# A perceiver block on one core: the first attention's maximum and sum spread by float32r matmuls, and weight buffers arranged anew

## The chip, the cores and the metric

The kernel runs on one core of one Trainium2 chip, in one launch. The core has TensorE (matmuls, written PE in the profile; PEld is its loading of the stationary operand), VectorE (DVE), ScalarE (ACT), GpSimd (POOL) and SyncE (SP), which issues the transfers here; each works through its own queue in order. The metric is the time of one execution on the device in microseconds (us). The kernel before takes 2688.52 us, the median of three runs (2685.12 to 2690.39).

## The reference

Two layers of three blocks each work on `x` (8 batches of 64 rows, 512 wide) and a context `ctx` (8 batches of 1601 rows, 512 wide), all in float32:

```python
x = x + xattn0(layernorm(x), ctx)   # 32 query heads, 8 key/value heads, head size 128, learned Wq, Wkv, Wo
x = x + mamba(layernorm(x))         # selective scan, 1024 channels, 16 states
x = x + ternary_ffn(layernorm(x))
x = x + xattn1(layernorm(x), ctx)   # softmax(x ctx^T) ctx, no weights
x = x + attn1(layernorm(x))         # causal self-attention, 32 heads of 16
x = x + oct_ffn(layernorm(x))       # gated, ternary octonion weights
```

The first block is where nearly all of the work lies. For a batch and one of the 8 key/value heads (a *unit* from here on) it is

```python
k, v   = ctx @ Wk + bk, ctx @ Wv + bv                 # 1601 x 128 each
scores = q @ k.T / sqrt(128)                          # 4 query heads x 64 rows = 256 queries
attn   = softmax(scores)                              # over 1601 keys
o      = attn @ v ;  out = o @ Wo + bo
```

## The kernel before

**Precision.** TensorE takes two kinds of four-byte operand here, float32 (`FP`) and float32r (`FR`), of the same size in memory. Where float32r is used, a value is kept as two float32r halves: `split` (L100) writes hi with a ScalarE copy that rounds, and lo = value - hi with VectorE or GpSimd. A product then has three terms (hi hi, hi lo, lo hi). Keys, values, scores and Wo are done so; the weighted sum over the values (L464), the maximum's spread (L412) and the sum's spread (L472) use plain float32.

**The main loop.** `x_all` (L517) goes through 64 units, batch by batch. Each unit has six steps. In them TensorE makes the keys of blocks of the context (`x_k`, L363) and the values of one tile of 128 context rows (`x_v`, L334), and the scores, transposed: keys on the partitions, the 256 queries along the free axis (`x_s`, L385). The softmax of a unit runs during the next unit's steps:

- `x_max` (step 0): the running maximum over the key tiles is transposed (L403), reduced by VectorE to one negative maximum per query (`col`, tile `mc`, L405).
- `x_spread` (step 0): two matmuls of 128 columns with `col` broadcast as the stationary side and the identity as the moving one bring each query's maximum to all partitions (L412).
- `x_exp` (steps 0 to 4, seven calls): VectorE adds the spread maximum to a pair of score tiles (L426), ScalarE takes the exponential (L427), GpSimd adds the pair to the running sum `ss` (L429, L452). The last call adds the short thirteenth tile (L446) and folds the two halves into `sl` (L448). For the very last unit (`flush`) VectorE does a part of it (L434 to L442).
- `x_av` (steps 2 to 5): the exponentials times the values, in plain float32 (L464).
- `x_o` (step 5): a matmul of 256 columns with a matrix of ones sums `sl` over the partitions and spreads the sum (L472); ScalarE and VectorE form the reciprocal (L474 to L477), scale (L479) and split the result.
- `x_wo`: for odd batches, the product with Wo (L511), weights fetched in four tiles per unit on the tag `wo` (three buffers).

The PSUM tag `kv` has four banks (`KVB`), shared by keys, values, scores and Wo; `o` and `m` have one each.

**The side work.** Beside the main loop run generators, advanced in step with it (`advance`, L1314): `halves` (L606) splits Wo, W_out and the attention weights once and stores the halves in HBM (56 tiles, during the first batch); `prep` (L620) makes ternary weights; and `chain` (L761), one for each group of two batches, does the other five blocks. While the main loop runs, what these issue on VectorE, ScalarE and GpSimd is kept in program order; the rest is ordered by the framework's scheduler, with its own model of durations. SyncE's queue issues the transfers in order, so a transfer that waits for a buffer holds those behind it.

**The tail.** The last group's chain starts when the main loop is done; the pools of the main loop and of the Mamba blocks (`ca`) are closed and their room is used by larger buffers (`BUFS_TAIL`), which wait for what was there. The third group's chain is still running then.

**Buffers that the diff touches** (`BUFS`, L46): `lv` (4 KB a partition) holds the Mamba block's u, dt and dus; `w2` (2 KB) single halves of weights for `mm3` (L742), which does the three terms; `b2` temporaries, among them the three pieces of a row of scores in `xattn1` (L1011), of 512, 512 and 578 columns; `b2` takes the size of the largest.

Of the kernel before, what the change touches and what calls it, by code (L numbers as in the profile page):

```python
# [16 lines left out]
P = 128  # L17
# [25 lines left out]
CPLAN = (0, 1, 2, None, None, 3)  # L43
AVPLAN = ((), (), (0, 1, 2, 3), (4, 5, 6, 7), (8, 9, 10, 11), (12,))
EXPLAN = ((0,), (1, 2), (3,), (4, 5), (6,), ())
BUFS = {"a2": 5, "lv": 3, "bc": 1, "xpad": 1, "b2": 5, "b4": 2, "w2": 3, "xr": 2}  # L46
BUFS_TAIL = {"a2": 6, "du": 2, "bc": 2, "xpad": 4, "s4": 11, "kb": 3, "b2": 8, "b4": 3, "w2": 12, "xr": 2}


# [29 lines left out]
class Kernel:  # L79
# [317 lines left out]
    def x_max(self, b, i):  # L397

        nc = self.nc
        m = self.mf.pop((b, i))  # L400
        ps = self.px.tile([P, 2, 256], FP, name=self.nm("m_ps"), tag="m", bufs=MB)
        for h in range(2):
            nc.tensor.transpose(ps[:, 0, h * P : (h + 1) * P], m[:, 0, h * P : (h + 1) * P], self.ident)  # L403
        col = self.sb("mc", [P, 2], pool=self.xp, bufs=2)
        nc.vector.tensor_reduce(col, ps[:, 0].rearrange("p (h k) -> p h k", k=P), AX.X, ALU.max, negate=True)  # L405
        self.mm[(b, i)] = (ps, col)

    def x_spread(self, b, i):

        ps, col = self.mm[(b, i)]  # L410
        for h in range(2):
            self.nc.tensor.matmul(  # L412
                ps[:, 1, h * P : (h + 1) * P], lhsT=col[:, h : h + 1].to_broadcast([P, P]), rhs=self.ident, start=True, stop=True
            )

    def x_exp(self, b, i, n):

        nc = self.nc
        ps = self.mm[(b, i)][0]
        S = self.S[(b, i)]  # L420
        if n == 0:
            self.ss[(b, i)] = self.sb("ss", [P, 2, 256], pool=self.xp, bufs=1)
        ss = self.ss[(b, i)]
        r, w = (P, 2) if n < 6 else (TAIL, 1)
        sv = S[n][:r, :w]
        nc.vector.tensor_tensor(sv, sv, ps[:r, 1:2].to_broadcast([r, w, 256]), ALU.add)  # L426
        nc.scalar.activation(sv, sv, AF.Exp, scale=ISC)  # L427
        if n == 1:
            nc.gpsimd.tensor_tensor(ss, S[0], S[1], ALU.add)  # L429
        elif n > 3 and self.flush:  # L430

            if n == 5:
                t = self.fs = self.sb("rw", [P, 256], pool=self.xp, bufs=1)
                nc.vector.tensor_tensor(t, S[4][:, 0], S[4][:, 1], ALU.add)  # L434
                for k in range(2):
                    nc.vector.tensor_tensor(t, t, S[5][:, k], ALU.add)
            elif n == 6:
                t = self.fs
                nc.vector.tensor_tensor(t[:r], t[:r], sv[:, 0], ALU.add)
                l = self.sb("sl", [P, 256], pool=self.xp, bufs=1)  # L440
                nc.vector.tensor_tensor(l, ss[:, 0], ss[:, 1], ALU.add)
                nc.vector.tensor_tensor(l, l, t, ALU.add)  # L442
                self.l[(b, i)] = l
                self.mm.pop((b, i))
        elif n == 6:
            nc.gpsimd.tensor_tensor(ss[:r, 0], ss[:r, 0], sv[:, 0], ALU.add)  # L446
            l = self.sb("sl", [P, 256], pool=self.xp, bufs=1)
            nc.gpsimd.tensor_tensor(l, ss[:, 0], ss[:, 1], ALU.add)  # L448
            self.l[(b, i)] = l
            self.mm.pop((b, i))  # L450
        elif n > 1:
            nc.gpsimd.tensor_tensor(ss, ss, S[n], ALU.add)  # L452
# [13 lines left out]
    def x_o(self, b, i):  # L466
# [2 lines left out]
        ps = self.o.pop((b, i))  # L469
        self.S.pop((b, i))  # L470
        r = self.l.pop((b, i))
        nc.tensor.matmul(ps[:, 1], lhsT=self.ones, rhs=r, start=True, stop=True)  # L472
# [19 lines left out]
    def x_wo(self, b, i):  # L492
# [113 lines left out]
    def halves(self):  # L606
# [2 lines left out]
        todo = [(i["Wo"][k * G + g], self.wo_s[k][:, g]) for k in range(NKV) for g in range(G)]  # L609
        todo += [(i["W_outT"][h], self.wout_s[h]) for h in range(NCH)]  # L610
        todo += [(i["attnT"][m, c], self.wat_s[m][c]) for m in range(4) for c in range(NC)]
        for src, dst in todo:
            t = self.sb("wo", [P, 2, D], FR, pool=self.xp, bufs=WOB)
            nc.sync.dma_start(out=t[:, 1].bitcast(FP), in_=src)
            yield 0.5
            self.split(t[:, 0], t[:, 1], t[:, 1].bitcast(FP), eng=nc.gpsimd)
            nc.sync.dma_start(out=dst, in_=t.bitcast(FP))
            yield 0.5

    def prep(self):  # L620
# [121 lines left out]
    def mm3(self, ps, lhsT, wt, N, start, stop, exact=False, tg="w2"):  # L742

        nc = self.nc
        if exact:
            wh = self.sb(tg, [P, D], FR)[:, :N]
            nc.sync.dma_start(out=wh.bitcast(FP), in_=wt)
        elif self.tail:
            w = self.sb(tg, [P, 2, D], FR)
            nc.sync.dma_start(out=w.bitcast(FP), in_=wt)  # L750
            wh, wl = w[:, 0], w[:, 1]
        else:
            wh, wl = (self.sb(tg, [P, D], FR) for _ in range(2))
            nc.sync.dma_start(out=wh.bitcast(FP), in_=wt[:, 0])
            nc.sync.dma_start(out=wl.bitcast(FP), in_=wt[:, 1])
        nc.tensor.matmul(ps, lhsT=lhsT(0), rhs=wh, start=start, stop=False)  # L756
# [240 lines left out]
    def xattn1(self, bs, x, xo):  # L997

        nc, i = self.nc, self.i
        lt = self.lnT(x, P, hl=False)  # L1000
        GW = [(0, (256, 256)), (1, (256, 256)), (2, (192, 192)), (2, (194,))]
        SW = [512, 512, 577]
        TS = ((0, 4), (4, 8), (8, NT))

        def scores(k, b):
# [2 lines left out]
                s = self.sb("bc", [T, LP])  # L1008
                S = [s[:, :512], s[:, 512:1024], s[:, 1024:]]
            else:  # L1010
                S = [self.sb("b2", [T, 512]), self.sb("b2", [T, 512]), self.sb("b2", [T, 578])]  # L1011
            o = 0
            for m, ws in GW:
                ps = self.acc()
# [20 lines left out]
                o += e  # L1035
                if not self.tail:
                    yield 2 * len(ws)
            nm = self.sb("s1m", [T, 4])
            for m in range(3):
                nc.vector.tensor_reduce(nm[:, m : m + 1], S[m][:, : SW[m]], AX.X, ALU.max)  # L1040
            nc.vector.tensor_reduce(nm[:, 3:4], nm[:, 0:3], AX.X, ALU.max, negate=True)
            sm2 = self.sb("s1s", [T, 4])
            for m in range(3):
                nc.scalar.activation(S[m][:, : SW[m]], S[m][:, : SW[m]], AF.Exp, bias=nm[:, 3:4], accum_out=sm2[:, m : m + 1])
            sm = sm2[:, 3:4]
            nc.vector.tensor_reduce(sm, sm2[:, 0:3], AX.X, ALU.add)
            nc.vector.reciprocal(sm, sm)
            yield 3
            return S, sm
# [1 line left out]
        def values(k, b, S, sm):  # L1051
            q0 = k * T
            pts = []
            for m, (t0, t1) in enumerate(TS):
                pt = self.sb("b2", [P, 5, T])
                tp = self.acc().rearrange("p (t q) -> p t q", q=T)
                for t in range(t0, t1):
                    r = rows_of(t)
                    nc.tensor.transpose(tp[:r, t - t0, :], S[m][:, (t - t0) * P : (t - t0) * P + r], self.ident[:T, :T])
# [225 lines left out]
    def run(self):  # L1285
# [3 lines left out]
        self.pc = ctx.enter_context(tc.tile_pool(name="pc", bufs=2, space=PSUM))  # L1289
        xctx = ctx.enter_context(ExitStack())  # L1290
        self.px = xctx.enter_context(tc.tile_pool(name="px", bufs=2, space=PSUM))
        self.consts()
        self.scratch()
        self.xw = ctx.enter_context(tc.tile_pool(name="xw", bufs=2))
# [74 lines left out]
HALVES_START = 0.1  # L1369
HALVES_END = 0.97  # L1370
HALVES_COST = 56.0
MAMBA_TAGS = ("a2", "lv", "bc", "xpad", "sm")
# [117 lines left out]
```

## Time and profile before

| | us |
|---|---|
| median of three runs | 2688.52 |
| the profiled execution, its own time | 2687.19 |
| its span, first to last instruction | 2685.1 |
| first attention's main loop, about | 0 to 2385 |
| tail | 2385 to 2685 |
| TensorE idle in the span | 135.4 |
| L412 (256 records), mean duration of one | 0.277 |
| L472 (128 records), mean duration of one | 0.380 |
| L464 (1664 records), mean duration of one | 0.381 |
| L334 (4992 records, float32r), mean duration of one | 0.281 |
| granted TensorE clock, mean share | 0.983 |

The span is read from the first line of the page, the busy times from its second part. A row of the groups gives line, engine, operation, output and inputs, shape and count, then busy time and mean duration in ns, then the engine's idle time just ahead of it and what ended it. Matmuls overlap in the pipeline, so a mean duration is longer than what an instruction costs; the timeline's distance from one start to the next is nearer to that. In a wait's line the first name is who waited, the second who released it, then the total in us, the number of times and the longest.

### The profile page before, as it was taken

What the parts mean: (1) busy time and instruction counts of PE and PEld (TensorE: products, weight loads), DVE (VectorE), ACT (ScalarE), POOL (GpSimd) and SP (SyncE); (2) the same over time, 40 slices, a digit from 0 to 9 for tenths busy, and PEclk for the clock granted to TensorE, in tenths of its full rate; (3) what the DMA queues carried; (4) which work ended last, traced back from release to release, by engine and by line L of the source; (5) the groups of instructions that cost most, each with busy time, mean ns of one, the idle gap of its engine ahead of it and who ended that gap; (6) DMA issues with size and microseconds to landing.
All of it is one profiled execution on the core that took longest, in us unless ns stands there. A gap on an engine that the chain in (4) does not pass through costs nothing.

```text
span 2685.1 us, 43976 instructions
## 1 busy us (share of the span) xinstructions
PE 2549.7 (95%) x16320; PEld 2269.3 (85%) x16320; DVE 1667.6 (62%) x2739; ACT 1350.2 (50%) x3128; POOL 1247.6 (46%) x1243
## 2 busy tenths in 40 slices
PE   7999999999999999999999999999999999977797
PEld 6988999999999899978989988988898898964544
DVE  4534357665687775545567676554657777668754
ACT  4545454344556554544555554544546545436433
POOL 2434463463368663521367457521239556405420
PEclk9999999999999999999999999999999999987899
DMA  9788876675213244764324452665343455466674
GB/s 308 225 295 276 281 239 190 203 240 180 67 66 105 68 133 150 232 190 145 97 98 148 149 161 89 216 201 164 102 135 92 137 159 155 143 226 216 234 261 166
DMA packets 311126, 466.08 MB, mean 174 GB/s; under 512 B 88440, under 2 KB 187768, under 8 KB 306432
## 3 DMA queue, kind: packets, MB, share of 16 engines
q1 hardware_dynamic: 310912, 463.28, 53.4%
q8 instruction: 128, 2.10, 0.3%
q14 instruction: 86, 0.70, 0.1%
HBM read 389.66 MB, written 73.53 MB: 173 GB/s over the span
## 4 chain that ended last, share of the span: by engine, by line
PE 68%; DMA 9%; DVE 9%; POOL 7%; issue 4%; ACT 3%; SPq 0%; POOLq 0%; DVEq 0%; ACTq 0%
PE v_ps L334 16%; PE k_ps L363 16%; PE o_ps L464 10%; PE s_ps L385 8%; POOL a L65 3%; PE w_ps L511 2%; PE acc L274 2%; DVE a L65 2%; PE acc L1077 2%; PE acc L801 2%; PE acc L1021 1%; PE acc L759 1%; PE acc L756 1%; POOL ss L452 1%; DMA b<-in_ctxT_dram 1%
## 5 line engine op out<-in xcount | busy, mean ns | idle before, releaser
L363 PE MATMUL k_ps<-cxb,wk 128*128 128x384 f32 x2304 | 470.3, 347 | 35.3 <-DVE mx L392 13.2
L334 PE MATMUL v_ps<-wv,cxb 128*128 128x256 f32 x3456 | 467.9, 281 | 1.0 <-DVE kt L109 0.6
L334 PEld LDWEIGHTS v_ps<-wv,cxb 128*128 128x128 f32 x3456 | 438.0, 188 | 19.3 <-issue 11.7
L363 PEld LDWEIGHTS k_ps<-cxb,wk 128*128 128x128 f32 x2304 | 405.3, 191 | 53.2 <-DVE mx L392 15.6
L464 PE MATMUL o_ps<-S,v 128*128 128x256 f32 (+1 forms) x1664 | 413.6, 381 | 7.4 <-DVE rw L479 4.0
L385 PE MATMUL s_ps<-q,kt 128*128 128x256 f32 (+1 forms) x2496 | 413.7, 299 | 5.2 <-DVE mx L392 2.4
L385 PEld LDWEIGHTS s_ps<-q,kt 128*128 128x128 f32 (+1 forms) x2496 | 342.8, 185 | 28.5 <-issue 6.9
L388 ACT COPY S<-s_ps 128x512 f32<-128x512 f32 (+1 forms) x448 | 241.9, 553 | 241.0 <-PE s_ps L385 236.6
L452 POOL TENSOR_TENSOR ss<-ss,S 128x512 f32<-128x512 f32 x254 | 349.3, 1375 | 14.7 <-ACT S L427 1.3
L392 DVE TENSOR_TENSOR mx<-s_ps,mx 128x512 f32<-128x512 f32 x256 | 175.1, 684 | 264.0 <-ACT S L388 262.7
L464 PEld LDWEIGHTS o_ps<-S,v 128*128 128x128 f32 (+1 forms) x1664 | 298.6, 190 | 46.7 <-issue 5.2
L429 POOL TENSOR_TENSOR ss<-S,S 128x512 f32<-128x512 f32 x64 | 84.5, 1320 | 469.4 <-ACT S L427 469.1
L108 ACT ACTIVATE kt<-k_ps,c_bk 128x384 fp32r<-128x384 f32 (+1 forms) x256 | 152.0, 594 | 246.9 <-PE k_ps L363 245.9
L426 DVE TENSOR_TENSOR S<-S,m_ps 128x512 f32<-128x512 f32 (+1 forms) x448 | 257.3, 640 | 20.5 <-PE m_ps L412 20.2
L427 ACT ACTIVATE S<-S 128x512 f32<-128x512 f32 (+1 forms) x448 | 246.7, 599 | 43.4 <-DVE S L426 42.7
L109 DVE SCALAR_TENSOR_TENSOR kt<-k_ps,c_bk,kt 128x384 fp32r<-128x384 f32 (+1 forms) x256 | 160.9, 629 | 158.0 <-ACT kt L108 156.5
L337 ACT COPY v<-v_ps 128x256 f32<-128x256 f32 (+1 forms) x416 | 152.5, 368 | 198.4 <-PE v_ps L334 196.0
L334 PE MATMUL v_ps<-wv,cxt 128*128 128x256 f32 (+1 forms) x1536 | 206.5, 282 | 1.5 <-DVE mx L392 1.0
L334 PEld LDWEIGHTS v_ps<-wv,cxt 128*128 128x128 f32 (+1 forms) x1536 | 192.7, 175 | 10.5 <-issue 3.4
L65 DVE TENSOR_TENSOR_SCAN a<-a,a 128x512 f32<-128x512 f32 x96 | 154.7, 1613 | 62.9 <-POOL a L65 62.8
L363 PE MATMUL k_ps<-cxt,wk 128*128 128x450 f32 x768 | 178.6, 375 | 1.4 <-DVE mx L392 1.3
L65 POOL TENSOR_TENSOR a<-a,bc 128x512 f32<-128x512 f32 x96 | 128.1, 1335 | 90.7 <-DVE a L65 90.7
(357 smaller groups left out, 3947.8 us busy)
## 6 DMA issues: line engine op xcount, KB each, us to landing
wo<-d_wo SPq DMA_DIRECT2D x128, 512.0 KB, 5.3
wk<-d_wk SPq DMA_DIRECT2D x63, 512.0 KB, 3.5
wv<-d_wv SPq DMA_DIRECT2D x31, 1024.0 KB, 5.7
cst<-in_ctxT_dram SPq DMA_DIRECT2D x96, 192.0 KB, 3.0
b<-in_ctxN_dram SPq DMA_DIRECT2D x36, 512.0 KB, 3.7
d_q<-q_t SPq DMA_DIRECT2D x32, 512.0 KB, 5.9
q<-d_q SPq DMA_DIRECT2D x64, 256.0 KB, 3.1
d_wo<-wo SPq DMA_DIRECT2D x32, 512.0 KB, 5.7
```

Source lines behind the costliest of these rows:

```text
L65: return lambda *a, **k: self.tc.keep_in_program_order(f(*a, **k))
L109: eng.scalar_tensor_tensor(lo, src, bias, hi.bitcast(FP), ALU.add, ALU.subtract)
L334: nc.tensor.matmul(ps[:r], lhsT=cx[:, a, c, o : o + r], rhs=w[:, m, c, :], start=k == 0, stop=k == 11)
L337: nc.scalar.copy(vt[:r], ps[:r])
L363: nc.tensor.matmul(ps[:, :wd], lhsT=w[:, a, c, :], rhs=cx[:, m, c, :], start=k == 0, stop=k == 11)
L385: nc.tensor.matmul(sp[:r, gi, :], lhsT=kt[:, a, o : o + r], rhs=q[:, m, :], start=k == 0, stop=k == 2)
L388: nc.scalar.copy(s[:r, :n], sp[:r, :n])
L392: nc.vector.tensor_tensor(mx, sp, S[0] if len(S) == 1 else mx, ALU.max)
L426: nc.vector.tensor_tensor(sv, sv, ps[:r, 1:2].to_broadcast([r, w, 256]), ALU.add)
L427: nc.scalar.activation(sv, sv, AF.Exp, scale=ISC)
L452: nc.gpsimd.tensor_tensor(ss, ss, S[n], ALU.add)
L464: nc.tensor.matmul(ps[:, 0], lhsT=self.v[(b, j, t)][:r, hc : hc + P], rhs=S[t // 2][:r, t % 2], start=t == 0, stop=t == NT - 1)
```

## The change

In the first attention:

- `col` (L404) is written as float32r, and the spread of the maximum (L412) becomes a float32r matmul with a float32r identity, `ident_r`. The maximum is thereby rounded; it is subtracted from every score alike.
- The folded sum `sl` is split into hi and lo in a new tile on the tag `ss`: a ScalarE copy, then a subtraction on GpSimd (on VectorE for the last unit). The sum's spread (L472) becomes two float32r matmuls of 256 columns with `ones_r`.
- The identity and the ones are float32r tiles, made by a copy from a temporary and from the identity; their float32 views serve all other uses.

In the weights and buffers:

- `halves` holds two tiles loaded ahead and issues the load of tile k + 2 behind the store of tile k.
- The fourth Wo tile of the very last `x_wo` takes the `wk` buffer.
- `w2` has four buffers in place of three. Of the three `lv` buffers two stay; u has one of its own, `lu`.
- `mm3` uses the low half of the weights last. With `pair` it fetches both halves in one transfer; `mamba_out` does so in the `lv` buffers while the main loop runs, and no longer on `w2`.
- `xattn1` ahead of the tail cuts a row of scores into 512, 512, 512 and 65 columns in place of 512, 512 and 577, so that `b2` shrinks to 512 columns; there is one more reduction and one more exponential for a batch. The transfers are six of 256 columns and one of 66, in place of four of 256, two of 192 and one of 194.

```diff
-BUFS = {"a2": 5, "lv": 3, "bc": 1, "xpad": 1, "b2": 5, "b4": 2, "w2": 3, "xr": 2}
+BUFS = {"a2": 5, "lv": 2, "lu": 1, "bc": 1, "xpad": 1, "b2": 5, "b4": 2, "w2": 4, "xr": 2}
@@ consts
-        self.ident = c.tile([P, P], FP, name="ident")
-        make_identity(nc, self.ident)
+        one = self.xw.tile([P, D], FP, name="one", tag="x1")[:, :P]
+        make_identity(nc, one)
+        self.ident_r = c.tile([P, P], FR, name="ident")
+        self.ident = self.ident_r.bitcast(FP)
+        nc.scalar.copy(self.ident_r, one)
...
-        self.ones = c.tile([P, P], FP, name="ones")
-        nc.gpsimd.memset(self.ones, 1.0)
+        self.ones_r = c.tile([P, P], FR, name="ones")
+        self.ones = self.ones_r.bitcast(FP)
+        nc.vector.tensor_scalar(self.ones_r, self.ident, 0.0, 1.0, ALU.mult, ALU.add)
@@ x_max, x_spread
-        col = self.sb("mc", [P, 2], pool=self.xp, bufs=2)
+        col = self.sb("mc", [P, 2], FR, pool=self.xp, bufs=2)
...
-                ps[:, 1, h * P : (h + 1) * P], lhsT=col[:, h : h + 1].to_broadcast([P, P]), rhs=self.ident, start=True, stop=True
+                ps[:, 1, h * P : (h + 1) * P], lhsT=col[:, h : h + 1].to_broadcast([P, P]), rhs=self.ident_r, start=True, stop=True
@@ x_exp (flush, n == 6)
                 nc.vector.tensor_tensor(l, l, t, ALU.add)
+                sr = self.ss[(b, i)] = self.sb("ss", [P, 2, 256], FR, pool=self.xp, bufs=1)
+                self.split(sr[:, 0], sr[:, 1], l)
@@ x_exp (n == 6)
             nc.gpsimd.tensor_tensor(l, ss[:, 0], ss[:, 1], ALU.add)
+            sr = self.ss[(b, i)] = self.sb("ss", [P, 2, 256], FR, pool=self.xp, bufs=1)
+            self.split(sr[:, 0], sr[:, 1], l, eng=nc.gpsimd)
@@ x_o
-        nc.tensor.matmul(ps[:, 1], lhsT=self.ones, rhs=r, start=True, stop=True)
+        sr = self.ss.pop((b, i))
+        for h in range(2):
+            nc.tensor.matmul(ps[:, 1], lhsT=self.ones_r, rhs=sr[:, h], start=h == 0, stop=h == 1)
@@ x_wo
-            w = self.sb("wo", [P, 2, D], FR, pool=self.xp, bufs=WOB)
+            last = (b, i, g) == (self.B - 1, NKV - 1, WOB)
+            w = self.sb("wk" if last else "wo", [P, 2, D], FR, pool=self.xp, bufs=1 if last else WOB)
@@ halves
-        for src, dst in todo:
-            t = self.sb("wo", [P, 2, D], FR, pool=self.xp, bufs=WOB)
-            nc.sync.dma_start(out=t[:, 1].bitcast(FP), in_=src)
+        ts = {}
+
+        def load(k):
+            if k < len(todo):
+                ts[k] = self.sb("wo", [P, 2, D], FR, pool=self.xp, bufs=WOB)
+                nc.sync.dma_start(out=ts[k][:, 1].bitcast(FP), in_=todo[k][0])
+
+        load(0)
+        load(1)
+        yield 1
+        for k, (src, dst) in enumerate(todo):
+            t = ts.pop(k)
+            self.split(t[:, 0], t[:, 1], t[:, 1].bitcast(FP), eng=nc.gpsimd)
             yield 0.5
-            self.split(t[:, 0], t[:, 1], t[:, 1].bitcast(FP), eng=nc.gpsimd)
             nc.sync.dma_start(out=dst, in_=t.bitcast(FP))
+            load(k + 2)
             yield 0.5
@@ mm3 (new argument pair=False)
-        elif self.tail:
+        elif self.tail or pair:
...
+        nc.tensor.matmul(ps, lhsT=lhsT(1), rhs=wh, start=False, stop=stop and exact)
         if not exact:
-            nc.tensor.matmul(ps, lhsT=lhsT(0), rhs=wl, start=False, stop=False)
-        nc.tensor.matmul(ps, lhsT=lhsT(1), rhs=wh, start=False, stop=stop)
+            nc.tensor.matmul(ps, lhsT=lhsT(0), rhs=wl, start=False, stop=stop)
@@ mamba, mamba_out
-        u = self.sb(self.tv, [P, NCH, 2, T])
+        u = self.sb(self.tv if tail else "lu", [P, NCH, 2, T])
...
-        self.mm3(ps, lambda a: yt[:, a, :], self.wout_s[c], D, c == 0, c == NCH - 1, tg=self.t4)
+        self.mm3(ps, lambda a: yt[:, a, :], self.wout_s[c], D, c == 0, c == NCH - 1, tg=self.tv if not self.tail else self.t4, pair=True)
@@ xattn1
-        GW = [(0, (256, 256)), (1, (256, 256)), (2, (192, 192)), (2, (194,))]
-        SW = [512, 512, 577]
+        if self.tail:
...
+        else:
+            GW = [(0, (256, 256)), (1, (256, 256)), (2, (256, 256)), (3, (66,))]
+            SW = [512, 512, 512, 65]
...
-                S = [self.sb("b2", [T, 512]), self.sb("b2", [T, 512]), self.sb("b2", [T, 578])]
+                S = [*(self.sb("b2", [T, 512]) for _ in range(3)), self.sb("s1x", [T, 66], bufs=1)]
```

More of the change, by code (lines that the diff above doesn't have):

```diff
@@ L740, in mm32, with mm3 @@
         self.nc.tensor.matmul(ps, lhsT=x, rhs=w, start=start, stop=stop)
-    def mm3(self, ps, lhsT, wt, N, start, stop, exact=False, tg="w2"):
+    def mm3(self, ps, lhsT, wt, N, start, stop, exact=False, tg="w2", pair=False):
         nc = self.nc
@@ L1000, in xattn1 @@
         lt = self.lnT(x, P, hl=False)
-        GW = [(0, (256, 256)), (1, (256, 256)), (2, (192, 192)), (2, (194,))]
-        SW = [512, 512, 577]
+        if self.tail:
+            GW = [(0, (256, 256)), (1, (256, 256)), (2, (192, 192)), (2, (194,))]
+            SW = [512, 512, 577]
+        else:
+            GW = [(0, (256, 256)), (1, (256, 256)), (2, (256, 256)), (3, (66,))]
+            SW = [512, 512, 512, 65]
+        NS = len(SW)
         TS = ((0, 4), (4, 8), (8, NT))
@@ L1037, in scores @@
                     yield 2 * len(ws)
-            nm = self.sb("s1m", [T, 4])
-            for m in range(3):
+            nm = self.sb("s1m", [T, 5])
+            for m in range(NS):
                 nc.vector.tensor_reduce(nm[:, m : m + 1], S[m][:, : SW[m]], AX.X, ALU.max)
[L1041 to L1046, printed above, removed]
+            nc.vector.tensor_reduce(nm[:, 4:5], nm[:, 0:NS], AX.X, ALU.max, negate=True)
+            sm2 = self.sb("s1s", [T, 5])
+            for m in range(NS):
+                nc.scalar.activation(S[m][:, : SW[m]], S[m][:, : SW[m]], AF.Exp, bias=nm[:, 4:5], accum_out=sm2[:, m : m + 1])
+            sm = sm2[:, 4:5]
+            nc.vector.tensor_reduce(sm, sm2[:, 0:NS], AX.X, ALU.add)
             nc.vector.reciprocal(sm, sm)
@@ L1058, in values @@
                     r = rows_of(t)
-                    nc.tensor.transpose(tp[:r, t - t0, :], S[m][:, (t - t0) * P : (t - t0) * P + r], self.ident[:T, :T])
+                    src = S[3][:, :r] if t == 12 and len(S) > 3 else S[m][:, (t - t0) * P : (t - t0) * P + r]
+                    nc.tensor.transpose(tp[:r, t - t0, :], src, self.ident[:T, :T])
                 e = min(t1, 12) - t0
@@ L1291, in run @@
         self.px = xctx.enter_context(tc.tile_pool(name="px", bufs=2, space=PSUM))
+        self.xw = ctx.enter_context(tc.tile_pool(name="xw", bufs=2))
         self.consts()
         self.scratch()
-        self.xw = ctx.enter_context(tc.tile_pool(name="xw", bufs=2))
         self.xp = xctx.enter_context(tc.tile_pool(name="xp", bufs=2))
@@ L1371 @@
 HALVES_COST = 56.0
-MAMBA_TAGS = ("a2", "lv", "bc", "xpad", "sm")
+MAMBA_TAGS = ("a2", "lv", "lu", "bc", "xpad", "sm")
 FFN_TAIL = (("l", 0), ("l", 1), ("a", 0), ("l", 2), ("a", 1), ("d", 0), ("a", 2), ("d", 1), ("d", 2))
```

## The prediction

> **What bounds the kernel now.** I read the head of the page first, then the chain that ended last, then the busy time by stretches of 67 us, then the groups of instructions by shape, and at last the timeline of TensorE at the places that the diff touches.
>
> ```profile
> span 2685.1 us, 43976 instructions
> PE 2549.7 (95%) x16320; PEld 2269.3 (85%) x16320; DVE 1667.6 (62%) x2739; ACT 1350.2 (50%) x3128; POOL 1247.6 (46%) x1243
> PE 68%; DMA 9%; DVE 9%; POOL 7%; issue 4%; ACT 3%; SPq 0%; POOLq 0%; DVEq 0%; ACTq 0%
> ```
>
> TensorE is busy for 95% of the span and makes 68% of the chain. That is a mean over two stages, so the stretches come next (start and end, length, then busy time of PE, PEld, DVE, ACT, POOL, the granted clock and the DMA share).
>
> ```profile
> 1273.00:1340.00 67.00, 67.00 (x449) 63.62 (x448) 37.69 (x74) 33.50 (x74) 21.19 (x18) 1.00 0.30 93
> 1608.00:1675.00 67.00, 60.51 (x379) 56.18 (x377) 46.78 (x64) 35.41 (x95) 50.42 (x55) 0.97 0.32 100
> 2412.00:2479.00 67.00, 48.00 (x284) 31.26 (x284) 53.18 (x90) 40.64 (x121) 31.77 (x32) 0.76 0.64 209
> ```
>
> The first line is the ordinary state of the first attention: TensorE never idles, so TensorE time taken away there is time gained. The second is one of the stretches in which the side chain's scans load VectorE and GpSimd, and TensorE loses 6.5 us of 67. From 67 to 2345 us there are 34 stretches; in six TensorE is below 63 us (those at 134, 871, 1541, 1608, 2077 and 2278). I count TensorE savings fully in 28 of 34 and as nothing in the six: a factor of 0.82. The third line lies in the tail, where TensorE is far from the bound.
>
> **The two float32r matmuls.** The groups by shape show what there is to save:
>
> ```profile
> L334 PE MATMUL v_ps<-wv,cxb 128*128 128x256 f32 x3456 | 467.9, 281 | 1.0 <-DVE kt L109 0.6 <-DVE mx L392 0.3
> L412 PE MATMUL m_ps<-ident,mc 128*128 128x128 f32 x256 | 40.0, 277 | 3.0 <-DVE mc L405 3.0
> L472 PE MATMUL o_ps<-sl,ones 128*128 128x256 f32 x128 | 38.2, 380 | 0.0
> ```
>
> There are 64 units (8 batches by 8 heads). The code calls L412 twice a unit and L472 once, so 128 and 64 matmuls, but the rows count 256 and 128: a plain float32 matmul is two instructions. The float32r ones of L334 are one each (32 head pairs by 13 tiles by 12 terms is 4992, the sum of its rows). The mean durations hold the pipeline's depth; what an instruction costs is the distance to the next start.
>
> ```profile
> 1034.90 0.84 PE L334 MATMUL v_ps<-wv,cxb 128*128 128x256 f32 x6
> 1035.58 0.60 PE L412 MATMUL m_ps<-ident,mc 128*128 128x128 f32 x4
> 1035.94 0.96 PE L334 MATMUL v_ps<-wv,cxb 128*128 128x256 f32 x6
> 1036.74 0.87 PE L385 MATMUL s_ps<-q,kt 128*128 128x256 f32 x6
> ...
> 1515.75 0.59 PE L472 MATMUL o_ps<-sl,ones 128*128 128x256 f32 x2
> 1515.99 1.05 PE L363 MATMUL k_ps<-cxb,wk 128*128 128x384 f32 x4
> 1516.88 0.39 PE L756 MATMUL acc<-w,b 128*128 128x512 f32 x1
> ...
> 1820.34 0.70 PE L1059 MATMUL acc<-ident,b 64*128 64x64 f32 x8
> 1820.97 0.73 PE L385 MATMUL s_ps<-q,kt 128*128 128x256 f32 x4
> ```
>
> Six L334 ahead of the spread take 0.68 us from start to start (0.113 each); the six behind it take 0.80, so the spread's last instruction runs some 0.09 us into them. The spread thus costs 0.36 + 0.09 = 0.45 us a unit. In the same way L472 costs 0.24 us up to L363's start, and L363's four take 0.89 instead of 4 x 0.175 = 0.70 (0.175 is its own distance inside a row): 0.24 + 0.19 = 0.43 us.
>
> The sum becomes two float32r matmuls of 256 columns, the shape of L334: 2 x 0.117 = 0.235 us. It saves 0.195 us a unit; over the 62 units ahead of the tail 12.1 us.
>
> The spread becomes two float32r matmuls of 128 columns. No row shows float32r with under 256 columns. The dear end: the mode gives nothing at this width, still 0.45 us, saving nothing. The cheap end: the eight L1059 transposes, of 64 columns with a stationary side as wide, start 0.63 / 8 = 0.079 us apart, so 2 x 0.079, saving 0.29 us. Half of L334's columns should not cost more than all (0.117), so I take 0.1 us each: 0.2 us for two, a saving of 0.25 us, over 62 units 15.5 us.
>
> A rule that speaks against this stands in the Trainium skill, "TensorE: Matmul & The Clock Gate", section "LDWEIGHTS (loading the stationary operand)": the load takes the stationary operand's columns over 1.2 GHz, 107 ns for 128, so a narrow matmul would wait for its weights. By that rule the spread would be 0.21 us and save 0.24 us a unit, 14.6 us in all; the L1059 row, 128 stationary columns every 79 ns, already goes below it.
>
> Together 27.6 us of TensorE time; by the factor 0.82, **22.7 us** reach the end.
>
> **The price: a longer road to the sum.** Today GpSimd adds the last exponentials (L446), folds the halves (L448), and L472 reads that. Now a ScalarE copy (hi) and a GpSimd subtraction (lo) stand between.
>
> ```profile
> 1506.58 2.64 POOL L452 TENSOR_TENSOR ss<-ss,S 128x512 f32<-128x512 f32 x2
> 1509.30 0.72 POOL L446 TENSOR_TENSOR ss<-ss,S 65x256 f32<-65x256 f32 x1
> 1510.10 0.73 POOL L448 TENSOR_TENSOR sl<-ss 128x256 f32<-128x256 f32 x1
> ```
>
> A copy of 128x256 is 0.37 us (L337's median), a subtraction 0.74 us (L448's median). With hand-overs and one instruction of 0.6 us ahead in ScalarE's queue that is 1.8 us. What hides it: from the end of L448 to the start of L472 I measured 63 distances in the trace; the median is 10.4 us, five are below 1.8 us (0.40, 0.77, 1.21, 1.23, 1.49). These five miss 3.9 us in all: **+3.9 us**. Without cover the whole 1.8 us would stand before each L472, and behind it in TensorE's order everything: 113 us. In busy time it is 63 x 0.74 = 47 us more on GpSimd (46% busy) and 24 us on ScalarE (50% busy), beside TensorE.
>
> The copy is a new wait of ScalarE on GpSimd. Behind it in ScalarE's queue stand the evictions of v_ps, k_ps and s_ps, for which TensorE waits once its four "kv" banks are full: four groups of L334, 4 x 12 x 0.117 = 5.6 us. From the last exponential (L427) to the end of L448 pass 7.8 us in the median, 4.8 in all but one at least. If the copy stood straight behind that exponential, TensorE would lose what exceeds 5.6 us: 203 us over the 52 units that do. If it stands where its input is ready, nothing. The order on the queue is the scheduler's choice and not in this trace; in it ScalarE's waits on GpSimd are few (the longest 2.1 us), so I take 1% of it: **+2 us**. GpSimd's own subtraction waits for that copy too, and the side chain's products queue behind it; GpSimd's busiest stretch of 67 us holds 60 us of work, and two units in it add 1.5 us.
>
> The sum's halves share the one "ss" buffer with the running sum, so the next unit's L429 must come after L472: it comes 8.0 us later at the least. Nothing.
>
> **Weights and buffers.** The preparation of the halves now loads two tiles ahead:
>
> ```profile
> SPq L614 <- DMA d_wo<-wo: 68.4, 27, 6.5
> SPq L617 <- POOL wo L65: 41.9, 27, 7.1
> ...
> PE k_ps L363 <- DMA wk<-d_wk: 9.2, 5, 4.1
> ```
>
> SyncE's queue stood 68.4 us behind stores before the next load and 41.9 us before stores; all 56 loads and 56 stores remain, so it is order, not traffic. In "w2" a fourth buffer shortens SyncE's standing for TensorE (114.2 us at L747, 94.7 us at L755). TensorE itself feels late transfers little: 9.2 us on wk in five waits. I take **-2 us**, with bounds of -9 (all of it) and +3 (the transfers of the main loop now meet earlier side loads). In mm3 the low half of the weights is used last, so its transfer may land a matmul later: nothing. mamba_out fetches 24 pairs of 512 KB instead of 48 halves of 256 KB, on the two buffers that dt and dus have left. The L1021 stage has as many columns and seven transfers a batch as before; one more reduction and exponential for six batches is some 6 x (0.4 + 0.3) us on VectorE and ScalarE (a 128x256 reduction is 0.42 us), not on the path. The identity's copy at the start ends before ScalarE's first work at 8.8 us: nothing.
>
> **The tail** (from 2385 us): the last x_wo no longer waits for a fourth "wo" buffer (TensorE idles 0.81 us there, and the chain holds a 7.53 us transfer of d_wout at 2366.9), while the last unit's sum gains a copy and a subtraction, 0.37 + 0.41 us. I take **-2 us**, bounds -8 and +8: the third group ends 13.4 us ahead of the last one (its output is issued at 2668.8, the last at 2682.1), so a shift that small is mostly hidden.
>
> **The sum:** -22.7 + 3.9 + 2 - 2 - 2 = -20.8 us against the profiled execution's own 2687.19 us (span 2685.1 us): 2666.4. The median of the runs, 2688.52, is 1.3 us higher, so **2668 us**. Own range 2645 to 2682: below by the cheap spread and both lower bounds, above by 14 us more of waits.
>
> **Rivals.**
> - *The spread saves nothing* at 128 columns. For it: no narrow float32r row exists. Against: the 79 ns row. Then 12.1 x 0.82 = 9.9 us are left and the sum is -8: 2680 us.
> - *The sum's copy holds ScalarE's queue* (the slower side). Place: behind the last exponential of a unit. Price: a share of the 203 us. It decides from 23 us, 11% of it; at a sixth (34 us) the time is 2688.5 - 22.8 + 34 = 2700 us. For it: GpSimd runs 7.8 us behind; against: ScalarE is free half the time and the copy may be put late.
> - *The tail takes it back*: the second-to-last chain's Mamba block ends at 2375.2 us, 9.6 us before the last x of the main loop. If it is bound by VectorE and GpSimd and does not come earlier, the tail's buffers wait for it: 20.8 - 9.6 = 11 us lost, 2679 us.
>
> **Chances.** Forecast 0.55, spread without gain 0.15, held queue 0.2, tail 0.1. What counts as no change is within 0.2%, 5.4 us. Faster: 0.53 + 0.11 + 0.06 = 0.70; slower: 0.18 of the held queue and 0.01 of the forecast, 0.19; the rest 0.11. The range reaches from the forecast's low end to the held queue at 2700.
>
> **What would show it.** L412's and L472's rows with 128 records each; the start distance behind L412 about 0.1 us; L472's idle time at a few us; ScalarE's wait of the new copy on GpSimd under 1 us a unit. The forecast is wrong if TensorE's idle before L334 and L363 grows by more than 20 us, with ScalarE named as releaser, or if the spread's two records still take 0.45 us from start to start.

## The result and the profile after

The changed kernel takes 2695.27 us, the median of twelve runs (2690.48 to 2705.50), beside 2688.57 us of the kernel before (2680.86 to 2692.30): a ratio of 1.0032, 95% interval 1.0018 to 1.0046. It is slower by 0.3%, where 2668 us had been forecast. The profiled execution is the slowest of the twelve, 2705.50 us, so some 10 of its 18 us over the profile before are its own.

The head of the page and the chain of the changed kernel:

```profile
span 2703.3 us, 43873 instructions
PE 2546.7 (94%) x16192; PEld 2265.6 (84%) x16192; DVE 1678.1 (62%) x2747; ACT 1372.5 (51%) x3205; POOL 1292.4 (48%) x1305
PE 64%; DVE 11%; POOL 9%; DMA 8%; issue 4%; ACT 3%; SPq 0%; POOLq 0%; DVEq 0%; ACTq 0%
```

128 matmul records are gone, yet TensorE's busy time fell by 3 us only; of its share of the chain, VectorE and GpSimd took over two points each. The two matmuls themselves did what was forecast. Their groups by shape, then TensorE's timeline around them:

```profile
L482 PE MATMUL o_ps<-ss,ones 128*128 128x256 f32 x128 | 28.8, 293 | 2.8 <-ACT ss L105 2.3 <-POOL ss L106 0.5
L416 PE MATMUL m_ps<-ident,mc 128*128 128x128 f32 x128 | 23.4, 263 | 6.6 <-DVE mc L409 6.6
```

```profile
642.59 0.39 PE L389 MATMUL s_ps<-q,kt 128*128 128x256 f32 x2
642.82 0.33 PE L416 MATMUL m_ps<-ident,mc 128*128 128x128 f32 x2
642.99 0.68 PE L389 MATMUL s_ps<-q,kt 128*128 128x256 f32 x4
643.51 0.84 PE L522 MATMUL w_ps<-wo,ot 128*128 128x512 f32 x3
...
1052.98 0.40 PE L482 MATMUL o_ps<-ss,ones 128*128 128x256 f32 x2
1053.22 1.04 PE L367 MATMUL k_ps<-cxb,wk 128*128 128x384 f32 x5
```

Each call is now one record. The spread takes 0.17 us to the next start, and the four L389 behind it 0.52 in place of 0.47: 0.22 us (before 0.45). The sum takes 0.24 us (before 0.43). Over 62 units that is 26 us.

The loads of the stationary operand show the same for the spread. Before, four of them take 0.45 us to the next load; after, two take 0.22:

```profile
1035.46 0.52 PEld L412 LDWEIGHTS m_ps<-ident,mc 128*128 128x128 f32 x4
1035.91 0.78 PEld L334 LDWEIGHTS v_ps<-wv,cxb 128*128 128x128 f32 x6
```

```profile
642.71 0.30 PEld L416 LDWEIGHTS m_ps<-ident,mc 128*128 128x128 f32 x2
642.93 0.54 PEld L389 LDWEIGHTS s_ps<-q,kt 128*128 128x128 f32 x4
```

Where it went shows when the span is cut at the end of the main loop, the last x of `x_wo` (columns as in the stretches above: length, busy time of PE, PEld, DVE, ACT, POOL, granted clock, DMA share). Before, and after:

```profile
0.00:2385.50 2385.50, 2311.13 (x14996) 2118.22 (x14997) 1472.22 (x2373) 1210.49 (x2757) 1159.18 (x1151) 0.99 0.52 167
2385.50:2685.10 299.60, 238.58 (x1325) 151.10 (x1324) 195.40 (x367) 139.74 (x371) 88.44 (x92) 0.89 0.67 229
```

```profile
0.00:2401.50 2401.50, 2327.89 (x15052) 2118.41 (x15054) 1494.41 (x2410) 1243.73 (x2866) 1204.91 (x1213) 0.99 0.53 170
2401.50:2703.30 301.80, 218.81 (x1142) 147.15 (x1138) 183.71 (x338) 128.75 (x339) 87.46 (x92) 0.81 0.56 188
```

The main loop holds 56 matmul records more, though 128 float32 ones were taken out: some 180 records of the side chains moved into it from the tail (1325 records there before, 1142 after). The tail, with less to do, is no shorter, and its clock fell from 0.89 to 0.81. Summing the distances to the next start over the side chains' matmuls in the main loop (all that write `acc`, without the queries' projection at the start; idle time is in it) gives 229.7 us before and 254.1 us after.

### The profile page after: what moved, and what is told of

Its sections match the earlier page's. It is cut to its first block, busy times and chain, and to the rows that moved or that the text cites. A ratio compares the mean times of both kernels' runs of the same rounds, so it can differ in the third digit from the quotient of the medians.

```text
span 2703.3 us, 43873 instructions
## 1 busy us (share of the span) xinstructions
PE 2546.7 (94%) x16192; PEld 2265.6 (84%) x16192; DVE 1678.1 (62%) x2747; ACT 1372.5 (51%) x3205; POOL 1292.4 (48%) x1305
## 4 chain that ended last, share of the span: by engine, by line
PE 64%; DVE 11%; POOL 9%; DMA 8%; issue 4%; ACT 3%; SPq 0%; POOLq 0%; DVEq 0%; ACTq 0%
PE v_ps L338 15%; PE k_ps L367 15%; PE o_ps L472 9%; PE s_ps L389 8%; POOL a L65 3%; DVE a L65 3%; PE w_ps L522 2%; PE acc L822 2%; POOL ss L460 2%; PE acc L1104 2%; PE acc L278 2%; PE acc L1047 2%; PE acc L777 1%; PE acc L778 1%; DVE b L65 1%
## 5 line engine op out<-in xcount | busy, mean ns | idle before, releaser
L367 PE MATMUL k_ps<-cxb,wk 128*128 128x384 f32 x2304 | 463.4, 344 | 30.8 <-ACT cxb L105 10.6
L389 PE MATMUL s_ps<-q,kt 128*128 128x256 f32 (+1 forms) x2496 | 416.1, 299 | 9.0 <-DVE kt L109 5.6
L472 PE MATMUL o_ps<-S,v 128*128 128x256 f32 (+1 forms) x1664 | 410.8, 380 | 1.8 <-ACT S L431 1.3
L389 PEld LDWEIGHTS s_ps<-q,kt 128*128 128x128 f32 (+1 forms) x2496 | 342.1, 185 | 36.5 <-issue 10.0
L472 PEld LDWEIGHTS o_ps<-S,v 128*128 128x128 f32 (+1 forms) x1664 | 298.9, 190 | 37.0 <-issue 3.2
L65 DVE TENSOR_TENSOR_SCAN a<-a,a 128x512 f32<-128x512 f32 x96 | 158.7, 1654 | 57.4 <-POOL a L65 57.3
L65 POOL TENSOR_TENSOR a<-a,bc 128x512 f32<-128x512 f32 x96 | 128.1, 1335 | 78.9 <-DVE a L65 78.9
```

What stands on the lines that cost most here:

```text
L65: return lambda *a, **k: self.tc.keep_in_program_order(f(*a, **k))
L367: nc.tensor.matmul(ps[:, :wd], lhsT=w[:, a, c, :], rhs=cx[:, m, c, :], start=k == 0, stop=k == 11)
L389: nc.tensor.matmul(sp[:r, gi, :], lhsT=kt[:, a, o : o + r], rhs=q[:, m, :], start=k == 0, stop=k == 2)
L472: nc.tensor.matmul(ps[:, 0], lhsT=self.v[(b, j, t)][:r, hc : hc + P], rhs=S[t // 2][:r, t % 2], start=t == 0, stop=t == NT - 1)
```

## Experiments

Each kernel ran on one chip beside the kernel before. Ratios are to it, with 95% intervals; the chips are not the same for all kernels, so differences between them are taken from the ratios. "Room" below is the part of the change in weights and buffers.

### The parts of the change

Four kernels carry one part each; the rest is as before. Their edits are these parts of the diff above:

```diff
# e1: float32r part, spread and sum   e3: the first two lines   e4: the last two   (all three with ident_r, ones_r)
+        col = self.sb("mc", [P, 2], FR, pool=self.xp, bufs=2)
...
+                ps[:, 1, h * P : (h + 1) * P], lhsT=col[:, h : h + 1].to_broadcast([P, P]), rhs=self.ident_r, start=True, stop=True
...
+            self.split(sr[:, 0], sr[:, 1], l, eng=nc.gpsimd)
...
+            nc.tensor.matmul(ps[:, 1], lhsT=self.ones_r, rhs=sr[:, h], start=h == 0, stop=h == 1)
# e2: room
+BUFS = {"a2": 5, "lv": 2, "lu": 1, "bc": 1, "xpad": 1, "b2": 5, "b4": 2, "w2": 4, "xr": 2}
...
```

> The kernel before with the float32r part alone: float32r identity and ones, the spread of the maximum and the sum's spread as float32r matmuls, the sum split into hi and lo. Weights and buffers as before. Theory A (the float32r part does what was forecast, and the weights and buffers move work of the third group's chain out of the tail, where it is hidden, into the main loop, where it is not): 15 to 22 us faster than the kernel before, some 2668 us, and the Mamba block of the third group ends near 2350 us as before. Theory B (the longer road to the sum holds ScalarE's queue and takes the gain back): within 5 us of the changed kernel, 2690 to 2700 us. Theory C (the lower granted clock follows from any shift in the schedule): about 2690 us, clock 0.975.

> The kernel before with the weights and buffers of the change alone (two tiles ahead in halves, the last Wo tile on wk, w2, lv and lu, pairs in mamba_out, the order in mm3, the cut of xattn1); the spread and the sum in plain float32 as before. Theory A: 15 to 30 us slower than the kernel before, 2705 to 2718 us, with the third group's chain 50 us or more ahead at the end of the main loop. Theory B: no slower than the kernel before, 2685 to 2690 us. Theory C: about 2695 us.

> The kernel before with the float32r spread of the maximum alone; the sum stays plain float32 without halves. TensorE's cost of the spread measured in the changed kernel is 0.22 us a unit in place of 0.45. Theory A and B: 64 x 0.22 = 14 us less TensorE time, 10 to 13 us faster, 2676 us. Theory C: anything between 2676 and 2695 us with the clock as the difference.

> The kernel before with the sum's halves and its two float32r matmuls alone; the spread stays plain float32. Theory A: 64 x 0.19 = 12 us less TensorE time, some of it lost to the copy, 4 to 10 us faster, 2680 us. Theory B: 10 us or more slower than the kernel before, 2699 us or above, with ScalarE's wait for the folded sum at 75 us and TensorE idle behind the evictions.

| | median us | ratio | main loop ends | third group's Mamba ends | tail's first projection | tail |
|---|---|---|---|---|---|---|
| before | 2688.6 | 1 | 2385.5 | 2375.9 | 2391.8 | 299.6 |
| changed | 2695.3 | 1.0032 (1.0018 to 1.0046) | 2401.5 | 2284.6 | 2408.7 | 301.8 |
| e1 float32r | 2692.6 | 1.0027 (1.0015 to 1.0039) | 2355.8 | 2378.3 | 2383.5 | 335.6 |
| e2 room | 2728.2 | 1.0155 (1.0133 to 1.0177) | 2424.8 | 2288.2 | 2431.7 | 298.5 |
| e3 spread | 2702.1 | 1.0059 (1.0040 to 1.0077) | 2368.6 | 2387.9 | 2393.3 | 333.5 |
| e4 sum | 2712.8 | 1.0097 (1.0077 to 1.0117) | 2372.5 | 2388.5 | 2393.6 | 339.1 |

(The ends are read from each profile's timeline: the last write of x, the first write of xr of that group, the first tail matmul of the input projection.) Every part alone is slower than nothing, and none took the time that Theory A gave: e2 went its way, but further. e1's time fits B and C, e4's fits B, though not in the way that B said; e3's fits none. (In the kernel before Mamba ends at 2375.9 us, not near 2350 as the text of e1 has it.) The main loop ended 30 us earlier with the float32r part, where 22.7 had been forecast, 17 and 13 us earlier with its halves, and 39 us later with the room. But each float32r kernel has a tail 34 to 40 us longer. The timeline at the joint, first of the kernel before (L514 the last x, L65 the Mamba block's result, L801 the projection), then of e1 (L524, L65, L811):

```profile
2375.24 0.69 DVE L65 TENSOR_TENSOR xr<-acc,x 128x512 f32<-128x512 f32 x1 [1.79 <-PE acc L759]
...
2384.83 0.69 DVE L514 TENSOR_TENSOR x<-w_ps,x 128x512 f32<-128x512 f32 x1 [0.47 <-PE w_ps L511]
...
2391.81 2.55 PE L801 MATMUL acc<-a,w 128*128 128x128 f32 x11
```

```profile
2355.09 0.69 DVE L524 TENSOR_TENSOR x<-w_ps,x 128x512 f32<-128x512 f32 x1 [9.89 <-PE w_ps L521]
...
2377.62 0.69 DVE L65 TENSOR_TENSOR xr<-acc,x 128x512 f32<-128x512 f32 x1 [11.20 <-PE acc L769]
...
2383.47 1.44 PE L811 MATMUL acc<-a,w 128*128 128x128 f32 x5
```

The last group's chain had its x at 2356 us, but its projections began at 2383, behind the third group's Mamba block; by the program, its buffers lie where that block's were. In the changed kernel it is the main loop that comes last:

```profile
2283.87 0.69 DVE L65 TENSOR_TENSOR xr<-acc,x 128x512 f32<-128x512 f32 x1 [1.14 <-PE acc L780]
...
2400.82 0.69 DVE L525 TENSOR_TENSOR x<-w_ps,x 128x512 f32<-128x512 f32 x1 [5.37 <-PE w_ps L522]
...
2408.71 2.50 PE L822 MATMUL acc<-a,w 128*128 128x128 f32 x10
```

### Which buffers, and the spacing of the third group

```diff
# e5: e1 with                  # e6: the changed kernel with
-SPAN = [3.1,3.1,2.6,0.2]      -SPAN = [3.1,3.1,2.6,0.2]
+SPAN = [3.1,3.1,2.4,0.2]      +SPAN = [3.1,3.1,3.0,0.2]
# e7: the changed kernel, halves and x_wo as before
# e8: e1 with the changed halves and x_wo
```

> e1_fr_only with one number more: the third group's chain is spread over 2.4 batches in place of 2.6 (SPAN), so its operations are issued earlier. In e1_fr_only the main loop ended 30 us earlier than before, the third group's Mamba block at 2377.6 us as before, and the tail grew by 36 us. Theory A2 (the end is set by the later of the main loop and the third group's Mamba block, with a tail of some 300 us behind it): Mamba ends some 25 us earlier, the main loop loses some 10 us to it, and the kernel takes 2660 to 2675 us. Theory B2 (the Mamba block is bound by VectorE and GpSimd whatever the order of issue): Mamba ends near 2375 us and the time stays at 2685 to 2695 us. Theory C2 (any shift of the schedule costs): 2690 to 2705 us.

> The changed kernel with the third group's chain spread over 3.0 batches in place of 2.6, so that its work comes later. In the changed kernel that Mamba block ended at 2284 us, 118 us ahead of the main loop, and the tail was no shorter for it (302 us, 300 before). Theory A2: Mamba ends some 55 us later, still ahead of the main loop; TensorE's side work in the main loop falls from 254 us towards 230, and the kernel takes 2672 to 2685 us. Theory B2: the same direction, some 2690 us. Theory C2: 2690 to 2705 us.

> The float32r part with the buffers of the side chain alone (w2, lv, lu, pairs in mamba_out, the order in mm3, the cut of xattn1); halves and the last Wo tile as before. Theory A2, if these buffers are what moves the side chain ahead: like the changed kernel, 2690 to 2700 us, with the second group's result stored near 2140 us. If halves is what moves it: like e1_fr_only, with that result near 2240 us.

> The float32r part with the two tiles ahead in halves and the last Wo tile on wk; the side chain's buffers as before. If the side chain's buffers are what moves the chain ahead: like e1_fr_only, 2690 us, the main loop's end within 8 us of 2356 us and the second group's result near 2240 us. If halves matters: the first 400 us are shorter by 3 us or more.

e5 took 2722.9 us (1.0120, 1.0106 to 1.0133): Mamba did not come earlier (2381 us), as B2 said, and the rest of the tail grew by 25 us, so that the time was worse than any theory's. e6 took 2676.2 us (0.9954, 0.9941 to 0.9967), faster than both kernels, as A2 said: the main loop ends at 2382.5 us with 235.8 us of side matmuls, the tail takes 288.6 us. Mamba came at 2296 us, 11 us later and not the 55 expected. Why the tail is 13 us shorter as well is not shown; the time lost there to a lower granted clock is 39 us in place of 57. e7 took 2708.9 us (1.0067, 1.0055 to 1.0079), 9 us above what was expected, the second group's result stored at 2143 us; e8 2688.7 us (0.9992, 0.9982 to 1.0002), that result at 2244 us and the main loop's end 4.5 us earlier than in e1. So the side chain's buffers, with the order in `mm3` and the cut of `xattn1`, move the chains 100 us ahead; which of these does it was not taken apart. By the ratios, `halves` and the last Wo tile take 9 us off, from e1 to e8 as from e7 to the changed kernel. One place where the chain gets ahead is the ternary block's four weights. TensorE in the kernel before:

```profile
1113.40 0.39 PE L756 MATMUL acc<-w,b 128*128 128x512 f32 x1
...
1115.27 0.39 PE L759 MATMUL acc<-w,b 128*128 128x512 f32 x1
1124.45 0.40 PE L756 MATMUL acc<-w,b 128*128 128x512 f32 x1
```

and in the changed one:

```profile
1093.96 0.40 PE L777 MATMUL acc<-w,b 128*128 128x512 f32 x1
...
1095.83 0.39 PE L777 MATMUL acc<-w,b 128*128 128x512 f32 x1
1096.06 0.39 PE L778 MATMUL acc<-w,b 128*128 128x512 f32 x1
```

With three `w2` buffers the fourth weight came 9.2 us behind the third; with four all are there within 2.5 us.

### The joint, and what the float32r part is worth

```diff
# SPAN's third number 3.0 in e9, e11, e12 and e16, 2.9 in e13, e14, e17, 3.3 in e10, e15, e18
# e10, e14: the changed kernel   e9, e17, e18: e2 (room alone)   e12: e1 (float32r alone)
# e11, e13, e15: room and the float32r spread; no halves of the sum
# e16: e6, but
-        for h in range(2):
-            nc.tensor.matmul(ps[:, 1], lhsT=self.ones_r, rhs=sr[:, h], start=h == 0, stop=h == 1)
+        nc.tensor.matmul(ps[:, 1], lhsT=self.ones, rhs=r, start=True, stop=True)
```

> e1_fr_only with the third group's chain over 3.0 batches in place of 2.6. In twelve profiles the tail's first projections began 5 to 7 us (in the kernel before 6.3 and 16.6) behind the later of two ends: the main loop's and the third group's Mamba block's. Theory A3: Mamba ends later than in e1_fr_only (2377.6 us), by 10 to 50 us, the projections begin 6 us behind it, and the time grows by as much: 2700 to 2740 us, while the main loop ends no later than 2356 us. Theory B3 (the Mamba block is not what holds the tail): the projections follow the main loop's end, 2685 to 2692 us.

e12 took 2711.0 us (1.0069, 1.0056 to 1.0082), as A3 said, though its main loop ended at 2365.5 us and not by 2356:

```profile
2364.81 0.69 DVE L524 TENSOR_TENSOR x<-w_ps,x 128x512 f32<-128x512 f32 x1 [0.50 <-PE w_ps L521]
...
2403.56 0.69 DVE L65 TENSOR_TENSOR xr<-acc,x 128x512 f32<-128x512 f32 x1 [12.29 <-PE acc L769]
...
2409.40 1.01 PE L811 MATMUL acc<-a,w 128*128 128x128 f32 x3
```

With Mamba put 26 us later the projections began 26 us later. In all twenty profiles they begin 4.4 to 10.3 us behind the later of the two ends.

> e6_after_span30 without the float32r part: spread and sum in plain float32, weights and buffers of the change, the third group's chain over 3.0 batches. It measures what the float32r part is worth once the third group's Mamba block ends ahead of the main loop. Theory A3 (the 26.5 us of TensorE time that the changed kernel's trace shows as saved reach the end there): 2676 + 18 to 27, that is 2694 to 2703 us. Theory B3 (the longer road to the sum and ScalarE's wait take most of it back): 2676 to 2686 us.

> The changed kernel with the third group's chain over 3.3 batches (3.0 in e6_after_span30). There Mamba ended at 2295 us, 87 us ahead of the main loop's end at 2382. Theory A3: Mamba ends later but still ahead, TensorE's side work in the main loop falls by another 5 to 15 us, the tail stays between 285 and 300 us: 2665 to 2678 us. Theory B3 (the tail's own order decides): the tail grows by what the main loop gains, 2676 to 2690 us.

> e6_after_span30 without the sum's halves: the spread in float32r, the sum's spread in plain float32 without the copy and the subtraction. Theory A3 (the sum's two matmuls are worth 64 x 0.19 = 12 us, of which the copy costs a few): 2681 to 2688 us. Theory B3 (the copy on ScalarE, which waited 75 us for GpSimd in the changed kernel, costs more than the matmuls give): 2676 us or below.

> e11_spread_room_span30 (spread in float32r, plain sum, the change's buffers) with the third group's chain over 2.9 batches. Theory A4 (the sum's halves cost some 10 us at every spacing): 2665 to 2680 us, and 6 to 15 us faster than e14. Theory B4 (the 10 us of e6 against e11 are the schedule's accident): the difference to e14 is under 5 us or of the other sign.

> The changed kernel with the third group's chain over 2.9 batches (3.0 in e6_after_span30, 2.6 in the changed kernel). Theory A4: 2676 to 2690 us, 6 to 15 us slower than e13. Theory B4: within 5 us of e13, or faster.

> e11_spread_room_span30 with the third group's chain over 3.3 batches, the partner of e10_after_span33 (2678.7 us). Theory A4: 2663 to 2673 us. Theory B4: 2674 us or above.

> e6_after_span30 with the sum's copy and subtraction made but not read: the sum is spread by one plain float32 matmul of the folded sum, as in e11. Theory A4 (ScalarE's wait for GpSimd and the two operations are the cost): slower than e11 by what the halves cost plus what the cheaper matmuls gave, 10 + 12 us, that is 2684 to 2692 us. Theory B4: within 8 us of e11, 2659 to 2675 us.

> The change's weights and buffers alone, plain float32 spread and sum, the third group's chain over 2.9 batches; the partner of e13 (2676.7 us) and e14 (2676.8 us). Theory A5 (the spread is worth the 14 us of TensorE time it frees, the halves of the sum nothing net): 2687 to 2695 us. Theory B5 (all of it is scatter between schedules): 2670 to 2684 us.

> The same with 3.3 batches; the partner of e15 (2674.8 us) and e10 (2678.7 us). Theory A5: 2685 to 2693 us. Theory B5: 2668 to 2682 us.

Medians in us, and ratios, with the room's buffers and Mamba ahead of the main loop's end:

| SPAN | plain | spread | spread and sum |
|---|---|---|---|
| 2.9 | e17 2684.2, 0.9984 (0.9975 to 0.9993) | e13 2676.7, 0.9955 (0.9943 to 0.9967) | e14 2676.8, 0.9951 (0.9939 to 0.9963) |
| 3.0 | e9 2688.7, 0.9991 (0.9981 to 1.0002) | e11 2666.5, 0.9905 (0.9889 to 0.9920) | e6 2676.2, 0.9954 (0.9941 to 0.9967) |
| 3.3 | e18 2677.5, 0.9961 (0.9946 to 0.9976) | e15 2674.8, 0.9955 (0.9941 to 0.9968) | e10 2678.7, 0.9954 (0.9939 to 0.9968) |

At one spacing one could have told any story. By the ratios the spread gives 23 us at 3.0, 8 at 2.9 and 2 at 3.3; the halves of the sum take 13 back at 3.0 and do nothing clear at 2.9 and 3.3. (e11 is B3's; e9 lies between the ranges of A3 and B3; e10's main loop ends 11 us earlier than e6's and its tail is 16 us longer, as B3 said.) Means over the rows are 0.9979, 0.9938 and 0.9953: 11 us for the spread, of 14 us of TensorE time, and -4 us for the halves of the sum. But schedules that differ in one number of spacing scatter by up to 13 us, so three differences of 23, 8 and 2 do not show a gain of 11. B4 held over A4. A5 failed twice; e18 lies within B5's range and e17 at its upper edge, so that the rows as a whole do not rule out B5, that all of it is scatter. At the spacing of 2.6, from e2 to the changed kernel, the float32r part is worth 33 us. e16 (copy and subtraction without their matmuls) took 2670.9 us (0.9933, 0.9921 to 0.9946), as B4 said: 7 us more than e11 by the ratios, within that scatter.

The fastest kernel is e11, 2666.5 us: the change without the sum's halves, the third group over 3.0 batches.

## Why the prediction was wrong

**The two matmuls: right.** Forecast 0.2 and 0.235 us a unit, measured 0.22 and 0.24. The Trainium skill's rule on the load of the stationary operand ("TensorE: Matmul & The Clock Gate", "LDWEIGHTS (loading the stationary operand)") gives an estimate of 107 ns for 128 columns. The spread's loads, 0.11 us each in this trace, agree with it better than with the 79 ns row that the prediction set against it. That row's stationary side is not "as wide" as its 64 columns; it has 128 columns, but 64 rows only.

**Weights and buffers, -2 us: the step that failed.** The term was given bounds of -9 and +3; alone (e2) the room costs 42 us by its ratio, 39 of them in the main loop. It was priced by what TensorE waited for. Its effect is on the side chains, which ran 100 us ahead and so put 34 us more of their matmuls into the main loop (229.7 us before, 263.4 in e2), where TensorE is the bound, out of a tail that stays near 299 us. `halves` and the last Wo tile are not to blame (9 us less in both pairs); the side chain's part is. In the changed kernel it met the float32r saving: from e2 to the changed kernel the main loop ends 23 us earlier, about the 22.7 forecast, but against the kernel before it still ends 16 us later, with 24 us more of side work. That the tail gains nothing by having less to do is measured, not explained.

**"22.7 us reach the end": failed too, where the float32r part stands without the room.** The saving did reach the end of the main loop, 30 us of it in e1. But the forecast took that loop's end for what the tail waits for. In the kernel before, the third group's Mamba block ends 9.6 us ahead of it; the first 10 us of saving make that block the last, and it did not come earlier in e1, e3, e4 and e5 (2378.3 to 2388.5 us). The rival "the tail takes it back" had the place and the condition; its price was 11 us, measured 36: in e1 the projections start 28 us behind the loop's end instead of 6, and the tail from there takes 15 us more. The third group's own blocks now end with the last group's (results issued at 2685.5 and 2688.4 us; before, 2668.8 and 2682.1); that this is what lengthens it is argued, and the lower clock (38 us lost from there on, before 33) is a rival for 5 of the 15. In the changed kernel itself the joint is cured: there the room put Mamba 117 us ahead.

**The longer road to the sum, +5.9 us: about right, and not all.** ScalarE's wait, from the waits of the changed kernel (total, times, longest):

```profile
ACT ss L105 <- POOL sl L454: 74.8, 47, 4.8
```

is 1.2 us a unit, over the 1 us that the forecast allowed. Yet e4's main loop ended 13 us earlier, so the held-queue rival did not decide. Nor did the forecast's own signs of being wrong come: TensorE's idle time before keys and values in the main loop is 36.5 us (39.2 before). They looked at TensorE's waits, and the loss lies in its work. Over the three spacings TensorE's idle time in the main loop has a mean of 67.7 us with the spread and 75.2 with the sum too: 7.5 us for the road. What was not forecast is the clock: the time lost to a lower granted clock there (length of each record times the share not granted) is 9.7 and 16.5 us. The 12 us of the sum's matmuls are so used up, roughly, as idle time and lower clock overlap in part: 12 - 7.5 - 6.8 = -2. That this edit's idle time brought the lower clock is argued from these sums; that the lower clock follows idle time is in the traces (last section).

**The range** held the time, but by luck: it reached beyond 2682 us for the held queue alone, which did not decide, and 0.19 was given to slower. Its low end does not come out either: the cheap spread and both lower bounds lead to about 2653 us, not 2645. What the scheduler's order alone does, up to 13 us between neighbours, is more than half of the gain forecast. That the changed schedule was one that had not been spaced again stands behind the result: with one number changed it is 12 us faster than the kernel before.

## What to carry to other kernels

A faster side chain is no gain if it carries work from a stage where an engine is idle into one where that engine is the bound; after such a change, space the side work anew before judging it. Before counting a saving on the busiest engine to the end, ask what else must be done at the point where the next stage starts: here two ends stood 9.6 us apart, and the second took all beyond that. Measure an edit at several neighbouring schedules: at one alone, the same edit gave 23 us or 2.

## What was not expected of the hardware

A float32r matmul of 128 columns cost 0.11 us, one of 256 columns 0.117: half the columns saved next to nothing. The spread's two matmuls start 0.06 us apart (median of 63), but their loads of the stationary operand take 0.225 us to the next load (median), and the four of plain float32 took 0.446. So what was saved is half of the loads.

TensorE's granted clock has two levels in these traces' main loops: full, and a share of 0.5 for 3.4 us or a multiple of it, mostly 3.4 or 6.8; in the profile before these cost 11.9 us there, in the changed one 22.2. The Trainium skill gives that length ("TensorE: Matmul & The Clock Gate", "Part 1: The HAM clock gate (the "warmup" mystery)"): a window of 3413 ns, and a clock halved after an idle one. The lengths agree; but the 3.4 us ahead need not be idle throughout. Ahead of all 134 such stretches in the twenty main loops TensorE was busy for 0 to 61% of that time.
